# Layer norm at the end of a graph network with experts: subtraction of the mean on GpSimd, part of the normalisation on VectorE, unequal groups

## The chip, the cores and the metric

The kernel runs on one core of a Trainium2 chip. The metric is the device time of one execution in microseconds (us). The engines are TensorE (PE), VectorE (DVE), ScalarE (ACT), GpSimd (POOL) and SyncE (SP), which issues most of the DMAs. Each engine works through its own queue in order and waits there for semaphores.

## The reference

One layer of a graph network: each node gathers its neighbours' rows, which are scaled by degrees and projected; a residual projection is added; a mixture of 64 experts, two for each node, is added to that; a batch norm over the nodes follows. The input is added again, and each row of 256 values is normalised. Cut to what matters here:

```python
def _layernorm(x, axis=-1, eps=1e-05):
    m = jnp.mean(x, axis=axis, keepdims=True)
    v = jnp.var(x, axis=axis, keepdims=True)
    return (x - m) / jnp.sqrt(v + eps)
...
    y = x + core                       # x: 6250 nodes of 256, core: the experts' part
    mean = jnp.mean(y, axis=0)
    var = jnp.mean((y - mean) ** 2, axis=0)
    return (y - mean) * jax.lax.rsqrt(var + BN_EPS) * gamma + beta
...
    x = _layernorm(x + _L0_gnn_ref(x, ...), axis=-1)
```

## The kernel before

The 6250 nodes lie in SBUF as 50 tiles (NT) of 125 partitions (TP) and 256 values (D), all in single precision: `x` is [125, 50, 256] and holds the layer's state, and `fb` of the same shape holds the layer's input. The kernel counts degrees and projects (to about 250 us), gathers and sums over edges (to about 1,240 us), routes to experts, runs the experts (to 1,890 us) and then the final stage. All stages but the last are the same before and after the change.

Some lines of the earlier stages appear in the prediction, since GpSimd and VectorE work at the same time there:

- L218 (VectorE, `hot_hi` and `hot_lo`): comparisons that build one-hot tables in bf16 from two tensors in SBUF.
- L338 and L432 (GpSimd, `hrow`): the difference of two 256-element rows per partition in SBUF.
- L449 to L451 (GpSimd, `mf`) and L454 to L457 (VectorE, `nmis`, `okd`): masks over edges, and two values that are reduced.
- L512, L544 and L576 (VectorE): comparisons with one or two scalars per partition.
- L956 (VectorE, `b1c`): a copy of four elements per partition for each expert.
- L1204 (GpSimd, `fb`): while the experts run, `beta` is added to `fb`, four tiles at a time, with beta's row repeated over the tiles.

The final stage is under a manual schedule: each engine runs its instructions in the order in which the program writes them. First, every two tiles, the experts' rows are loaded, VectorE adds them to `x` (L1248), ScalarE squares (L1251), and TensorE sums rows and squares over the nodes (L1253, L1255). From these sums VectorE makes `scale` (gamma over the deviation) and `less` (mean times scale), rows of 256 values that are the same on every partition (L1257 to L1267).

What follows is the part that is changed. The batch norm and the second residual are `x * scale + (fb - less)`; beta is in `fb` already. Before the change ten groups of five tiles go through three functions:

- `sums`: VectorE multiplies five tiles of `x` by `scale` (L1274), subtracts `less` from five tiles of `fb` (L1275), and adds the two tile by tile with the row sum as a second result (L1278). L1280 turns the sums `lm` into minus the row's mean.
- `squares`: ScalarE squares each row with the mean taken off and sums it (L1287), then takes a root for all five (L1289), `ssq`.
- `rows_out`: VectorE takes reciprocals (L1294) and the products with the means (L1295); ScalarE writes the normalised rows into the tile `o` (L1298); SyncE stores `o` in two DMAs, of 112 and of 13 partitions (`node_dma`, L139 to L141).

`rows_out` of a group stands behind `squares` of the next group. `o` comes from a pool of two buffers, `lm` and `ssq` have three.

Of the kernel before, what the change touches and what calls it, by code (L numbers as in the profile page):

```python
# [15 lines left out]
AF = mybir.ActivationFunctionType  # L16
ALU = mybir.AluOpType
# [7 lines left out]
TP = 125  # L25
NT = N // TP
D = 256
# [94 lines left out]
def gnn_moe_kernel(ctx, tc, x_in, src, dst, bases, firsts, slots, W_gc, b_gc, W_res, b_res, Wg, bg, w1, b1, w2, b2,  # L122
                   gamma, beta, out):
    nc = tc.nc
    V, S, G, T = nc.vector, nc.scalar, nc.gpsimd, nc.tensor
# [6 lines left out]
    def node_rows(ap, t0, n):  # L132
        return ap[t0 * TP:(t0 + n) * TP, :].rearrange("(t p) d -> p t d", p=TP)

    def node_dma(eng, to_sbuf, tile_ap, rows):

        for a, b in ((0, 112), (112, TP)):
            if to_sbuf:
                eng.dma_start(out=tile_ap[a:b], in_=rows[a:b])  # L139
            else:  # L140
                eng.dma_start(out=rows[a:b], in_=tile_ap[a:b])  # L141
# [55 lines left out]
    with tc.tile_pool(name="edges", bufs=1) as ep, ExitStack() as later:  # L197
# [30 lines left out]
        with tc.tile_pool(name="deg", bufs=1) as dp, tc.tile_pool(name="hot", bufs=2) as hp, \  # L228
# [52 lines left out]
            for a, b in ((0, HEAD), (HEAD, NGR)):  # L281
                floor_div(hi[:, a:b], srcf[:, a:b], TP)
                V.scalar_tensor_tensor(lo_b[:, a:b], hi[:, a:b], -float(TP), srcf[:, a:b], op0=ALU.mult,
                                       op1=ALU.add)
# [201 lines left out]
        with tc.tile_pool(name="cnt", bufs=1) as cp, tc.tile_pool(name="rows", bufs=1) as rp, \  # L486
# [44 lines left out]
            groups = [(c, j, i) for c, (g0, k, w, n) in enumerate(DENSE) for j in range(n) for i in range(k)]  # L531
# [219 lines left out]
            now, n = 0.0, 0  # L751
# [18 lines left out]
            with tc.For_i(0, n_groups, 1) as gi:  # L770
# [4 lines left out]
                                op1=ALU.mult)  # L775
# [3 lines left out]
                                       op0=ALU.mult, op1=ALU.add)  # L779
# [53 lines left out]
    x = xpool.tile([TP, NT, D], F32, name="x")  # L833
# [42 lines left out]
    with tc.tile_pool(name="xw", bufs=1) as xw, tc.tile_pool(name="xl", bufs=3) as xl, \  # L876
# [23 lines left out]
        with tc.manual_schedule():  # L900
            sums = {}
            for t0 in range(ta, tb, 2):
                n = min(2, tb - t0)
# [5 lines left out]
            for t0, z in sums.items():  # L909
                n = min(2, tb - t0)  # L910
# [6 lines left out]
                for t in range(t0, t0 + n):  # L917
                    V.scalar_tensor_tensor(x[:, t, :], z[:, t - t0, :D], s_in[:, t - t0:t - t0 + 1], x[:, t, :],
                                           op0=ALU.mult, op1=ALU.add)
# [7 lines left out]
            for a, b in ((0, ta), (tb, NT)):  # L927
                for t0 in range(a, b, 10):
                    n = min(10, b - t0)
# [37 lines left out]
    for j in range(2):  # L967
        o = rt.tile([TP, E, NT], BF16, name=f"pick{j}")
# [19 lines left out]
    with tc.tile_pool(name="ps_r", bufs=1, space=PSUM) as ps_r:  # L988
# [21 lines left out]
        for e0 in range(0, E, EC):  # L1010
            n = min(EC, E - e0)
# [21 lines left out]
        for a, m, r in ((0, LA, rest), (LA, LB, rest1)):  # L1033
# [10 lines left out]
                               accum_out=lb)  # L1044
# [4 lines left out]
                               accum_out=lb)  # L1049
# [37 lines left out]
    with tc.tile_pool(name="rt2", bufs=2) as rt2, \  # L1087
# [6 lines left out]
        for t0 in range(0, NT, TB):  # L1094
            for j in range(2):
# [13 lines left out]
                for i in range(TB):  # L1109
                    t = t0 + i  # L1110
# [23 lines left out]
    fb = fpool.tile([TP, NT, D], F32, name="fb")  # L1134
# [4 lines left out]
    with tc.tile_pool(name="ex", bufs=2) as xp, \  # L1139
# [56 lines left out]
        for e, r in enumerate(turns):  # L1196
            if e % 4 == 2:
                t0 = e // 4 * 4
                n = min(4, NT - t0)
# [6 lines left out]
            if e % 4 == 0 and e // 4 * 4 < NT:  # L1206
                xs = x[:, e:min(e + 4, NT), :]
# [3 lines left out]
            c, n = r + min(r, TWO), 2 if r < TWO else 1  # L1211
# [22 lines left out]
    with tc.tile_pool(name="fin", bufs=1) as fp, tc.tile_pool(name="gat", bufs=8) as gp, \  # L1234
            tc.tile_pool(name="fl", bufs=2) as fl, \
            tc.tile_pool(name="ps_m", bufs=1, space=PSUM) as ps_m, tc.manual_schedule():
        eps = fp.tile([TP, 2], F32, name="eps")
        V.memset(eps, LN_EPS)

        S.activation(eps[:, 1:2], eps[:, 0:1], AF.Sqrt)  # L1240
        pm = ps_m.tile([TP, D], F32, name="pm")
        pv = ps_m.tile([TP, D], F32, name="pv")
        for t0 in range(0, NT, 2):
            yr = gp.tile([TP, 2, 2, D], F32, name="yr")
            node_dma(nc.sync, True, yr.rearrange("p t j d -> p t (j d)"), node_rows(y_rows, t0, 2))
            for t in range(t0, t0 + 2):
                for j in range(2):
                    V.scalar_tensor_tensor(x[:, t, :], yr[:, t - t0, j, :], gates[:, j, t:t + 1], x[:, t, :],  # L1248
                                           op0=ALU.mult, op1=ALU.add)
            sq = fl.tile([TP, 2, D], F32, name="sq", bufs=4)  # L1250
            S.activation(sq, x[:, t0:t0 + 2, :], AF.Square)  # L1251
            for t in range(t0, t0 + 2):
                T.matmul(pm, ones[:TP, :TP], x[:, t, :], start=(t == 0), stop=(t == NT - 1))  # L1253
            for t in range(t0, t0 + 2):
                T.matmul(pv, ones[:TP, :TP], sq[:, t - t0, :], start=(t == 0), stop=(t == NT - 1))  # L1255
        mean = fp.tile([TP, D], F32, name="mean")
        V.tensor_scalar(mean, pm, 1.0 / N, None, op0=ALU.mult)  # L1257
        msq = fp.tile([TP, D], F32, name="msq")
        V.tensor_mul(msq, mean, mean)
        scale = fp.tile([TP, D], F32, name="scale")  # L1260
        V.scalar_tensor_tensor(scale, pv, 1.0 / N, msq, op0=ALU.mult, op1=ALU.subtract)
        V.tensor_scalar(scale, scale, 0.0, BN_EPS, op0=ALU.max, op1=ALU.add)
        S.activation(scale, scale, AF.Sqrt)
        V.reciprocal(scale, scale)  # L1264
        V.tensor_mul(scale, scale, gam)
        less = fp.tile([TP, D], F32, name="less")
        V.tensor_mul(less, mean, scale)  # L1267


        part = {}  # L1270

        def sums(t0):
            xs, fs = x[:, t0:t0 + 5, :], fb[:, t0:t0 + 5, :]
            V.tensor_tensor(xs, xs, scale[:, None, :].to_broadcast([TP, 5, D]), ALU.mult)  # L1274
            V.tensor_tensor(fs, fs, less[:, None, :].to_broadcast([TP, 5, D]), ALU.subtract)  # L1275
            lm = fl.tile([TP, 5], F32, name="lm", bufs=3)
            for t in range(5):
                V.scalar_tensor_tensor(xs[:, t, :], xs[:, t, :], 1.0, fs[:, t, :], op0=ALU.mult, op1=ALU.add,  # L1278
                                       accum_out=lm[:, t:t + 1])
            V.tensor_scalar(lm, lm, -1.0 / D, None, op0=ALU.mult)  # L1280
            part[t0] = lm

        def squares(t0):
            ssq = fl.tile([TP, 5], F32, name="ssq", bufs=3)
            for t in range(5):
                sq = fl.tile([TP, D], F32, name="sq2")
                S.activation(sq, x[:, t0 + t, :], AF.Square, bias=part[t0][:, t:t + 1],  # L1287
                             accum_out=ssq[:, t:t + 1])
            S.activation(ssq, ssq, AF.Sqrt, scale=1.0 / D, bias=eps[:, 0:1])  # L1289
            part["ssq", t0] = ssq  # L1290

        def rows_out(t0):
            rs, lm = part.pop(("ssq", t0)), part.pop(t0)
            V.reciprocal(rs, rs)  # L1294
            V.tensor_mul(lm, lm, rs)  # L1295
            o = fl.tile([TP, 5, D], F32, name="o")
            for t in range(5):
                S.activation(o[:, t, :], x[:, t0 + t, :], AF.Identity, scale=rs[:, t:t + 1], bias=lm[:, t:t + 1])  # L1298
            node_dma(nc.sync, False, o, node_rows(out, t0, 5))

        for t0 in range(0, NT, 5):
            sums(t0)
            squares(t0)
            if t0:
                rows_out(t0 - 5)
        rows_out(NT - 5)


_INS = ["x", "src", "dst"] + ["L0_gnn_" + n for n in (
# [44 lines left out]
```

## Time and profile before

| What | Before |
|---|---|
| Time, median of 3 runs | 2028.05 us (2023.2 to 2032.3) |
| The profiled execution: its time | 2020.97 us |
| The profiled execution: its span | 2019.2 us |
| Busy: PE, DVE, ACT, POOL | 1623.9, 1105.0, 756.7, 1024.7 us |
| First L1274 starts | 1954.31 us |
| Last L1298 ends (ACT) | 2013.96 us |

Times in the profile are counted from the span's start. The span is a little shorter than the time of the same execution, which has work around it, and this execution was faster than the median of the runs. A row of a group gives line, engine, operation, output and inputs with shapes, the count, and then busy time, the mean duration of one in ns, and the idle time before them. A row of the timeline gives start, duration, engine, line, operation; the brackets at its end give the idle time of the engine before it and what ended that. A row of the chain gives start, length and the piece of work. A row of busy times by stage gives the stretch, its length, the busy time of PE, weight loads, DVE, ACT and POOL, the granted clock of TensorE, the share of DMA and GB/s.

### The profile page before, as it was taken

Reading aid. Unit: us, or ns where it says so; the run is one execution under the profiler, and the core shown is the slowest. Engines: PE = TensorE matmul, PEld = TensorE weight load, DVE = VectorE, ACT = ScalarE, POOL = GpSimd, SP = SyncE. Lnnn points to the kernel's source line nnn. Section 1 sums busy time; section 2 is a strip of 40 time slices with the busy share of each in tenths; the row PEclk is TensorE's granted clock in tenths of the full one; section 3 lists DMA queues with packets and bytes.
Section 4 is the critical chain, followed back from the end, with each engine's and each line's share of the span. In section 5 each row is a group of like instructions: output and inputs, shape, how many; then the busy total and the mean of one; then the engine's idle time right before and its main releaser. Section 6 shows DMA issues by size and latency. Waiting matters only on the chain. (4 is left out here: it accounts for less than half of the span.)

```text
span 2019.2 us, 31796 instructions
## 1 busy us (share of the span) xinstructions
PE 1623.9 (80%) x10841; PEld 1359.8 (67%) x10841; DVE 1105.0 (55%) x2689; ACT 756.7 (37%) x1844; POOL 1024.7 (51%) x1099
## 2 busy tenths in 40 slices
PE   4999588888888888888878886359989999999760
PEld 2555457777777777878777775247778887778640
DVE  7999786665665654555554543983212221212497
ACT  1443554344434444444444442022222222223238
POOL 3433447667676666666656673015555555444100
PEclk9999679999999999998989987579999999999885
DMA  4765766777777776777766764907878887779754
GB/s 134 202 183 173 232 178 177 210 203 196 197 203 219 196 209 196 208 196 210 201 198 193 210 189 119 198 22 227 243 227 250 259 263 231 239 231 323 206 130 127
DMA packets 237970, 404.23 MB, mean 200 GB/s; under 512 B 26247, under 2 KB 155671, under 8 KB 237803
## 3 DMA queue, kind: packets, MB, share of 16 engines
q0 software_dynamic: 63584, 201.44, 35.3%
q1 hardware_dynamic: 166657, 193.19, 32.5%
q10 hardware_dynamic: 7562, 7.52, 1.4%
q8 instruction: 87, 1.43, 0.3%
q14 instruction: 80, 0.66, 0.1%
HBM read 324.36 MB, written 77.68 MB: 199 GB/s over the span
## 5 line engine op out<-in xcount | busy, mean ns | idle before, releaser
L502 POOL DMA_INDIRECT r<-h_dram,srcg x631 | 648.8, 1028 | 327.4 <-issue 114.2
L572 PE MATMUL sm<-hrow,counts 125*126 125x258 f32 (+2 forms) x1600 | 512.8, 338 | 4.9 <-issue 4.8
L573 PE MATMUL sm<-hrow,counts 125*126 125x256 f32 (+2 forms) x1600 | 436.1, 290 | 2.7 <-issue 2.5
L544 DVE TENSOR_SCALAR hotk<-iota_h,key 128x350 bf16<-128x350 f16 (+6 forms) x932 | 257.3, 315 | 324.6 <-PE pc L553 152.1
L557 ACT CAST stage<-pc 128x350 f16<-128x350 f32 (+6 forms) x666 | 278.4, 450 | 413.2 <-PE pc L553 210.0
L572 PEld LDWEIGHTS sm<-hrow,counts 125*126 125x126 f32 (+2 forms) x1600 | 321.5, 201 | 71.5 <-issue 65.2
L553 PE MATMUL pc<-hotk,lo 128*128 128x350 bf16 (+6 forms) x932 | 273.3, 333 | 68.2 <-issue 48.9
L573 PEld LDWEIGHTS sm<-hrow,counts 125*126 125x126 f32 (+2 forms) x1600 | 319.2, 200 | 3.7 <-issue 2.6
L1180 ACT ACTIVATE hT<-ph,b1c 128x256 f32<-128x256 f32 (+1 forms) x320 | 136.2, 429 | 395.6 <-PE ph L1178 217.7
L1178 PE MATMUL ph<-xgT,w1s 128*128 128x256 f32 (+1 forms) x1280 | 254.5, 346 | 25.9 <-DVE xgT L1173 13.2
L1178 PEld LDWEIGHTS ph<-xgT,w1s 128*128 128x128 f32 x1280 | 202.5, 192 | 71.4 <-ACT hT L1180 21.5
L1184 PE MATMUL py<-w2s,hT 128*128 128x256 f32 x1008 | 236.2, 384 | 5.0 <-ACT hT L1180 3.2
L507 PE MATMUL pg<-r,hot 128*128 128x258 f32 x631 | 212.6, 337 | 24.2 <-issue 9.7
L1188 POOL DMA_INDIRECT y_dram<-ys,dest x126 | 123.9, 983 | 175.5 <-DVE ys L1187 134.4
L1184 PEld LDWEIGHTS py<-w2s,hT 128*128 128x128 f32 x1008 | 189.9, 192 | 33.5 <-ACT hT L1180 5.5
L1168 POOL DMA_INDIRECT xg<-x_dram,ids x126 | 123.0, 976 | 160.6 <-DVE ids L1123 93.8
L508 PE MATMUL pg<-r,hot 128*128 128x256 f32 x631 | 183.1, 290 | 2.1 <-issue 1.9
L956 DVE COPY b1c<-b1T 128x4 f32 x80 | 17.7, 221 | 251.7 <-ACT hT L1180 214.0
L507 PEld LDWEIGHTS pg<-r,hot 128*128 128x128 f32 x631 | 127.1, 201 | 41.8 <-issue 17.6
L1187 DVE TENSOR_TENSOR ys<-py,b2s 128x256 f32<-128x256 f32 x126 | 53.4, 425 | 155.8 <-PE py L1184 121.4
L218 DVE TENSOR_TENSOR hot_lo<-lo_b,iota 128x4096 bf16<-128x4096 bf16 x49 | 130.9, 2671 | 0.0
L508 PEld LDWEIGHTS pg<-r,hot 128*128 128x128 f32 x631 | 126.9, 201 | 2.6 <-issue 1.5
(317 smaller groups left out, 2114.8 us busy)
## 6 DMA issues: line engine op xcount, KB each, us to landing
w1s<-in_L_gnn_w_dram SPq DMA_DIRECT2D x80, 512.0 KB
w2s<-in_L_gnn_w_dram SPq DMA_DIRECT2D x80, 512.0 KB
y_dram<-zeros SPq DMA_DIRECT2D x48, 256.0 KB
yr<-y_dram SPq DMA_DIRECT2D x25, 448.0 KB
b2s<-in_L_gnn_b_dram SPq DMA_DIRECT2D x80, 128.0 KB
r<-h_dram,srcg POOLq DMA_INDIRECT x631
h_dram<-hrow SPq DMA_DIRECT2D x5, 1344.0 KB
z_dram<-zeros ACTq DMA_DIRECT2D x7, 903.0 KB
```

Of the source, the lines that this page charges most:

```text
L218: V.tensor_tensor(o, pairs(t, c0, n, m), iota_2[:, None, :m, :].to_broadcast([128, n // 2, m, 2]), ALU.is_equal)
L502: G.indirect_dma_start(out=f32(r[:, :2 * D]), out_offset=None, in_=h_dram[:, :], in_offset=bass.IndirectOffsetOnAxis(ap=idx, axis=0))
L507: T.matmul(pg, hot, r[:, D:], start=first, stop=False)
L508: T.matmul(pg[:, :D], hot, r[:, :D], start=False, stop=last)
L544: V.tensor_scalar(hots[g], iota_h[:, :NT * w], key[:, g:g + 1], None, op0=ALU.is_equal)
L553: T.matmul(live["pc"], los[g // PAIRS][:, r // 2, :, r % 2], hots.pop(g), start=(i == 0), stop=(i == k - 1))
L557: S.copy(stage[:, :, j * w:(j + 1) * w], live["pc"])
L572: T.matmul(sm[:m], by, hrow[:, t, D:], start=(t == 0), stop=False)
L573: T.matmul(sm[:m, :D], by, hrow[:, t, :D], start=False, stop=(t == NT - 1))
L1178: T.matmul(ph[:, :m], w1s[:, kk, c * 128:(c + 1) * 128], xgT[:, kk, :m], start=(kk == 0), stop=(kk == 1))
L1180: S.activation(hT[:, c, :m], ph[:, :m], AF.Gelu, bias=b1_e[:, c:c + 1])
L1184: T.matmul(py, hT[:, c, k * 128:(k + 1) * 128], w2s[:, c, :], start=(c == 0), stop=(c == 3))
```

## The change

The groups have 2, 3, then eight times 5, then 3 and 2 tiles. The subtraction of `less` goes to GpSimd, and all twelve groups' subtractions are queued there at the start. The multiplication by `scale` of a group is written a group ahead of its sums. In a group, tiles with an odd number (two of five, one of three, one of two) are normalised on VectorE, the others on ScalarE as before. Nothing else differs.

```diff
-        def sums(t0):
-            xs, fs = x[:, t0:t0 + 5, :], fb[:, t0:t0 + 5, :]
-            V.tensor_tensor(xs, xs, scale[:, None, :].to_broadcast([TP, 5, D]), ALU.mult)
-            V.tensor_tensor(fs, fs, less[:, None, :].to_broadcast([TP, 5, D]), ALU.subtract)
+        groups, t0 = [], 0
+        for n in [2, 3] + [5] * ((NT - 10) // 5) + [3, 2]:
+            groups.append((t0, n))
+            t0 += n
+        assert t0 == NT
+
+        def residual(t0, n):
+            fs = fb[:, t0:t0 + n, :]
+            G.tensor_tensor(fs, fs, less[:, None, :].to_broadcast([TP, n, D]), ALU.subtract)
+
+        def scaled(t0, n):
+            xs = x[:, t0:t0 + n, :]
+            V.tensor_tensor(xs, xs, scale[:, None, :].to_broadcast([TP, n, D]), ALU.mult)
+
+        def sums(t0, n):
             lm = fl.tile([TP, 5], F32, name="lm", bufs=3)
-            for t in range(5):
-                V.scalar_tensor_tensor(xs[:, t, :], xs[:, t, :], 1.0, fs[:, t, :], op0=ALU.mult, op1=ALU.add,
-                                       accum_out=lm[:, t:t + 1])
+            for t in range(n):
+                V.scalar_tensor_tensor(x[:, t0 + t, :], x[:, t0 + t, :], 1.0, fb[:, t0 + t, :], op0=ALU.mult,
+                                       op1=ALU.add, accum_out=lm[:, t:t + 1])
...
-        def rows_out(t0):
+        def rows_out(t0, n):
             rs, lm = part.pop(("ssq", t0)), part.pop(t0)
-            V.reciprocal(rs, rs)
-            V.tensor_mul(lm, lm, rs)
+            V.reciprocal(rs[:, :n], rs[:, :n])
+            V.tensor_mul(lm[:, :n], lm[:, :n], rs[:, :n])
             o = fl.tile([TP, 5, D], F32, name="o")
-            for t in range(5):
-                S.activation(o[:, t, :], x[:, t0 + t, :], AF.Identity, scale=rs[:, t:t + 1], bias=lm[:, t:t + 1])
-            node_dma(nc.sync, False, o, node_rows(out, t0, 5))
-
-        for t0 in range(0, NT, 5):
-            sums(t0)
-            squares(t0)
-            if t0:
-                rows_out(t0 - 5)
-        rows_out(NT - 5)
+            for t in range(n):
+                if t % 2:
+                    V.tensor_scalar(o[:, t, :], x[:, t0 + t, :], rs[:, t:t + 1], lm[:, t:t + 1], op0=ALU.mult,
+                                    op1=ALU.add)
+                else:
+                    S.activation(o[:, t, :], x[:, t0 + t, :], AF.Identity, scale=rs[:, t:t + 1],
+                                 bias=lm[:, t:t + 1])
+            node_dma(nc.sync, False, o[:, :n, :], node_rows(out, t0, n))
+
+        for t0, n in groups:
+            residual(t0, n)
+        scaled(*groups[0])
+        for i, g in enumerate(groups):
+            if i + 1 < len(groups):
+                scaled(*groups[i + 1])
+            sums(*g)
+            squares(*g)
+            if i:
+                rows_out(*groups[i - 1])
+        rows_out(*groups[-1])
```

`squares` differs only in that it runs over n tiles.

More of the change, by code (lines that the diff above doesn't have):

```diff
@@ L1270, in gnn_moe_kernel, with squares @@
         part = {}
-        def sums(t0):
-            xs, fs = x[:, t0:t0 + 5, :], fb[:, t0:t0 + 5, :]
-            V.tensor_tensor(xs, xs, scale[:, None, :].to_broadcast([TP, 5, D]), ALU.mult)
-            V.tensor_tensor(fs, fs, less[:, None, :].to_broadcast([TP, 5, D]), ALU.subtract)
+        groups, t0 = [], 0
[10 more added lines that the diff above has]
+        def sums(t0, n):
             lm = fl.tile([TP, 5], F32, name="lm", bufs=3)
-            for t in range(5):
-                V.scalar_tensor_tensor(xs[:, t, :], xs[:, t, :], 1.0, fs[:, t, :], op0=ALU.mult, op1=ALU.add,
-                                       accum_out=lm[:, t:t + 1])
-            V.tensor_scalar(lm, lm, -1.0 / D, None, op0=ALU.mult)
+            for t in range(n):
+                V.scalar_tensor_tensor(x[:, t0 + t, :], x[:, t0 + t, :], 1.0, fb[:, t0 + t, :], op0=ALU.mult,
+                                       op1=ALU.add, accum_out=lm[:, t:t + 1])
+            V.tensor_scalar(lm[:, :n], lm[:, :n], -1.0 / D, None, op0=ALU.mult)
             part[t0] = lm
-        def squares(t0):
+        def squares(t0, n):
             ssq = fl.tile([TP, 5], F32, name="ssq", bufs=3)
-            for t in range(5):
+            for t in range(n):
                 sq = fl.tile([TP, D], F32, name="sq2")
@@ L1288, in squares @@
                              accum_out=ssq[:, t:t + 1])
-            S.activation(ssq, ssq, AF.Sqrt, scale=1.0 / D, bias=eps[:, 0:1])
+            S.activation(ssq[:, :n], ssq[:, :n], AF.Sqrt, scale=1.0 / D, bias=eps[:, 0:1])
             part["ssq", t0] = ssq
-        def rows_out(t0):
+        def rows_out(t0, n):
             rs, lm = part.pop(("ssq", t0)), part.pop(t0)
-            V.reciprocal(rs, rs)
-            V.tensor_mul(lm, lm, rs)
+            V.reciprocal(rs[:, :n], rs[:, :n])
+            V.tensor_mul(lm[:, :n], lm[:, :n], rs[:, :n])
             o = fl.tile([TP, 5, D], F32, name="o")
-            for t in range(5):
-                S.activation(o[:, t, :], x[:, t0 + t, :], AF.Identity, scale=rs[:, t:t + 1], bias=lm[:, t:t + 1])
-            node_dma(nc.sync, False, o, node_rows(out, t0, 5))
-        for t0 in range(0, NT, 5):
-            sums(t0)
-            squares(t0)
-            if t0:
-                rows_out(t0 - 5)
-        rows_out(NT - 5)
+            for t in range(n):
+                if t % 2:
[16 more added lines that the diff above has]
+        rows_out(*groups[-1])
 _INS = ["x", "src", "dst"] + ["L0_gnn_" + n for n in (
```

## The prediction

> **What bounds the kernel now.** I read the chain that ended last first, because only its last stretch runs through the changed lines; then busy times by stage; then, for the work that moves to GpSimd, the groups by form and the timeline at places where GpSimd and VectorE ran together. The first fence is from the chain (start, length, piece). One round of five tiles on VectorE goes from 1993.32 to 1998.54, 5.22 us; one round on ScalarE from 1985.26 to 1990.51, 5.25 us. The chain hops between two engines that are equally long.
>
> ```profile
> 1985.26 2.47 ACT sq L1287 x10
> ...
> 1987.75 0.04 ACT ssq L1289
> ...
> 1987.95 2.55 ACT o L1298 x5
> 1990.51 2.47 ACT sq L1287 x10
> ...
> 1993.32 1.83 DVE x L1278 x10
> 1995.17 0.17 DVE lm L1280
> 1995.34 0.10 DVE ssq L1294
> 1995.46 0.17 DVE lm L1295
> 1995.63 1.40 DVE x L1274
> 1997.03 1.42 DVE fb L1275
> ```
>
> The stages say the same: in 30 us VectorE works 29.06 and ScalarE 29.67, GpSimd nothing, and DMA has room (share 0.38).
>
> ```profile
> 1964.00:1994.00 30.00, 0.00 (x0) 0.00 (x0) 29.06 (x83) 29.67 (x93) 0.00 (x0) 0.50 0.38 107
> ```
>
> So the stage (first L1274 at 1954.31 to the span's end at 2019.2, 64.9 us) gets shorter only if both engines lose work and nothing takes its place. The question is what the idle engine charges. Its nearest rows, by form:
>
> ```profile
> L1204 POOL TENSOR_TENSOR fb<-fb,bet 125x1024 f32<-125x1024 f32 x12 | 28.2, 2354 | 12.7 <-DMA fb<-in_x_dram 12.6
> L1204 POOL TENSOR_TENSOR fb<-fb,bet 125x512 f32<-125x512 f32 x1 | 1.3, 1260 | 5.9 <-DMA fb<-in_x_dram 5.9
> ```
>
> It is the same shape of operation, with a row repeated over tiles: (2354 - 1260) / 512 = 2.14 ns per element and 0.17 us fixed. And the timeline shows what VectorE does meanwhile:
>
> ```profile
> 227.39 3.48 POOL L451 TENSOR_TENSOR mf<-mf,dstf 128x1568 f32<-128x1568 f32 x1
> 227.51 0.15 DVE L456 TENSOR_SCALAR okd<-okd 128x1 f32<-128x1 f32 x1
> 227.70 3.19 DVE L457 TENSOR_TENSOR nmis<-nmis,okd 128x1 f32<-128x1 f32 x1
> ...
> 96.00 0.98 DVE L218 TENSOR_TENSOR hot_hi<-hi_b,iota 128x1600 bf16<-128x1600 bf16 x1
> 96.37 1.20 POOL L338 TENSOR_TENSOR hrow<-whole,hrow 125x256 fp32r<-125x256 f32 x1 [2.44 <-ACT whole L337]
> 96.90 2.82 DVE L218 TENSOR_TENSOR hot_lo<-lo_b,iota 128x4096 bf16<-128x4096 bf16 x1
> ```
>
> L457 subtracts one element per partition from another and takes 3.19 us: it ends at 230.89, when GpSimd's L451 ends (230.87). L456, without a second tensor, passes in 0.15. In the second piece GpSimd's L338 takes 1.20 us, where its twin L432 has a median of 0.73 in a quieter stage: it stands until hot_hi ends at 96.98, then runs to 97.57, and hot_lo, started at 96.90, is stretched. With the rounds 3.55 and 3.64 us long in turn, and 0.90 for hot_hi and 2.20 for an undisturbed hot_lo (shortest 2.28, less the 0.08 by which neighbours overlap), one 256-element instruction on GpSimd costs VectorE 0.45 to 0.54 us. Two tensor operations of two SBUF inputs, one on each engine, exclude each other.
>
> **The change, part by part**, on the profiled execution (span 2019.2, time 2020.97; the median of the runs is 2028.05, and I add the difference of spans to that median).
>
> *VectorE's own work.* The fb subtraction leaves: 5.22 - 1.42 = 3.80 us per five tiles, 38.0 for fifty. Twelve groups in place of ten repeat twice what a group pays whatever its size: reciprocal and product 0.29, the scaling of lm with the gaps around the sums 0.38, a start 0.08; 1.5 in all. Twenty tiles are normalised here (two of five, one of two, one of three). The trace has no 256-element row with two scalars per partition. Below stands L1262 (two constants, 0.29, so 0.21 apart when overlapped), above L1248 (one scalar and a second tensor, 0.45 apart); L576, two scalars per partition on 128 elements, has a mean of about 0.34-0.38. I take 0.35, near L576: 7.0 (4.2 to 9.0). Sum 46.5 us, against 52.2 for ten rounds now.
>
> *ScalarE.* Fifty squares of 0.494, twelve roots at about 0.30 with their gaps, thirty normalisations of 0.493: 24.7 + 3.6 + 14.8 = 43.1 against 52.5 now. It stays just below VectorE's 46.5.
>
> *GpSimd.* Twelve subtractions over 12,800 elements per partition: 27.4 us of streaming and 12 x 0.17 = 2.0 fixed, 29.4 altogether. If it ran beside VectorE all of it would be free: it has nothing else here, and the first residual (1.26) is covered by the two scalings ahead (0.6 + 0.9). But x times scale (L1274) and the sums (L1278) read two SBUF tensors each, like L457 and hot_lo. So the streaming is added to VectorE's line. Its price there: L338's 0.45 to 0.54 per 256 elements gives 22.5 to 27; no hiding gives 29.4; no exclusion gives 0. I take 27.4 less about 0.1 for each of twelve hand-overs, in which VectorE's parts without a second tensor pass: 26.2. It is nearest to the row of L451 and L457, where the hold was complete.
>
> The Trainium skill, page "SBUF — State Buffer", section "Who interferes with whom", speaks against this change: it says that the port pair which GpSimd and VectorE share is held for the whole instruction. By that rule the term would be an estimated 29.4, and the sum 3.2 higher; the L338 rows say that a little of each instruction is free.
>
> *Order.* All residuals are queued at once, so they do not wait for VectorE's data, only for the port. L338 got in between two VectorE instructions, so I expect turns: for some 27 + 6 = 34 us one two-input instruction of VectorE per residual, the third group barely begun, ScalarE mostly idle. It can't make that up later: from the third group on it has about 40 of its 43 us left, which just fits behind 1988 in VectorE's line and the tail below.
>
> *The ends.* VectorE's line: 1954.31 + 46.5 + 26.2 = 2027.0. The last sums end before the normalisation work of the last two groups (2 x 0.65): 2025.7, against 2005.8 now. After that now: 13.4 us. Then: squares of two tiles 1.0, root 0.3, normalisations 1.5, gaps 0.6, and a store that is shorter: the span ends 5.2 us after ScalarE's last row (2013.96), of which three fifths of 2.7 us traffic go, leaving 3.6. Together 7.0. One new wait: `o` has two buffers, so the final two-tile group writes the buffer of the last five-tile group, whose store isn't done. Three of that group's rows (1.5 us with a gap 1.6) still stand on ScalarE when the last sums end; now traffic ends 3.5 us after the rows, and I add 1.0 for completion (0 to 1.7, by the span's end); then half a microsecond for the last row and 3.6 for its store: 1.6 + 4.5 + 0.5 + 3.6 = 10.2. I take that; without the wait it is 7.0.
>
> Sum: 2025.7 + 10.2 = 2035.9, 16.7 later than 2019.2. By parts: VectorE's own work -5.7, the port +26.2, the tail -3.2, and -0.6 because 1.3 of VectorE's line now lies behind the last sums where 0.7 does so today. Forecast: 2028.05 + 16.7 = 2044.8 us.
>
> **Rivals.** *A, no exclusion for these operations, so not slower.* Price: the 26.2 go away; 2009.7 for the span, -9.5, 2018.6. For it: no row has two long fp32 instructions of this kind at once. Against: L457 is an fp32 subtraction of two SBUF tensors and stood still; L956, a copy of 4 elements that normally takes 0.17, took 2.13 under the first L1204. It decides the sign where a GpSimd tile costs VectorE under 9.5 / 50 = 0.19 us; measured are 0.45 to 0.54. *B, GpSimd keeps the port through its whole queue*: VectorE stands for 29.4 with nothing hidden; +19.9, 2047.9. For it: L449, L450 and L451 follow each other within 0.1 us. Against: the turns at L338. *C, half the price* (0.25 per tile, 12.5): +3.0, 2031.1, if single-precision sums leave gaps that GpSimd can fill; no row shows such gaps.
>
> **How the numbers follow.** A measurement of this kernel can tell about 0.5%, 10 us, from no change: faster is below 2017.9, slower above 2038.2. Chances: forecast 0.70, B 0.13, C 0.06, A 0.11. The forecast's own range takes the low prices together (port 22.5, normalisations 4.2, no buffer wait: +7.0, 2035) to the high ones (29.4, 9.0: +22, 2050). The runs before lie 9 us apart, so I widen it to 2032 to 2052, which takes in B; A, most of C and scatter are left out, about 0.2. Slower: 0.60 of the forecast and B, 0.73. Same: 0.10 of the forecast, C and half of A, 0.21. Faster: the rest of A, 0.06.
>
> **What would show it.** Right: residuals on GpSimd stretched over some 34 us with a mean clearly above 2.9 us for five tiles; L1278 and L1274's successors with single instructions of about 3 us in that stretch and 0.42 and 1.48 afterwards; ScalarE with long waits for lm until about 1988, then rounds of 4.3 to 4.5 us; a wait of 2 to 3 us before the last rows for the store. Wrong: residuals at 2.9 us on end beside sums of 0.42 us (A), VectorE at rest for 29 us on end (B), normalisations on VectorE far from 0.4 us, or ScalarE rounds above 4.6 us.

## The result and the profile after

The changed kernel takes 2052.19 us (median of 4 runs, 2045.39 to 2062.23), the kernel before 2028.33 on the same chip: a ratio of 1.0102, interval 1.0066 to 1.0139. In us that is 20.7 slower, 13 to 28 (the two medians lie 23.9 apart); 16.7 had been forecast. The profiled execution has a span of 2049.8 us against 2019.2, 30.6 more, and that difference has two parts. The first multiplication by `scale` starts at 1968.3 instead of 1954.3, so 14.0 us were lost ahead of the final stage, where both kernels run the same program. The final stage itself, from that instruction to the span's end, takes 81.5 us against 64.9: 16.6 us longer.

The busy times of the final stage, in three stretches (columns as before: length, PE, weight loads, DVE, ACT, POOL, clock, DMA share, GB/s):

```profile
1968.30:2002.00 33.70, 0.00 (x0) 0.00 (x0) 33.56 (x23) 3.87 (x13) 33.31 (x12) 0.50 0.03 8
2002.00:2038.30 36.30, 0.00 (x0) 0.00 (x0) 34.03 (x137) 34.07 (x112) 0.00 (x0) 0.50 0.41 117
2038.30:2049.80 11.50, 0.00 (x0) 0.00 (x0) 2.96 (x13) 6.12 (x19) 0.00 (x0) 0.50 0.59 167
```

For 33 us GpSimd and VectorE both count as busy all the time, and yet VectorE gets 23 instructions done and ScalarE works for under 4 us. In the next 36 us VectorE does 137. An engine that is busy by the profile may be standing inside an instruction; the counts tell. The groups by form show where (first one of the kernel before, then those of the change):

```profile
L1278 DVE SCALAR_TENSOR_TENSOR x<-x,fb 125x256 f32<-125x256 f32 x50 | 18.1, 423 | 0.8
```

```profile
L1289 DVE SCALAR_TENSOR_TENSOR x<-x,fb 125x256 f32<-125x256 f32 x50 | 31.5, 686 | 0.0
L1280 POOL TENSOR_TENSOR fb<-fb,less 125x1280 f32<-125x1280 f32 x8 | 25.0, 3152 | 0.0
L1284 DVE TENSOR_TENSOR x<-x,scale 125x1280 f32<-125x1280 f32 x8 | 13.5, 1683 | 0.0
L1310 DVE TENSOR_SCALAR o<-x,ssq,lm 125x256 f32<-125x256 f32 x20 | 10.1, 537 | 5.6 <-DMA out_dram<-o 5.2
```

The mean of the sums is 0.69 us where it was 0.42, and a five-tile subtraction takes 3.15 us where 2.9 had been worked out for GpSimd alone. The timeline of the first stretch tells how a mean of 0.69 comes about:

```profile
1968.43 33.31 POOL L1280 TENSOR_TENSOR fb<-fb,less 125x512 f32<-125x512 f32 x12 [62.99 <-DVE less L1267]
...
1975.89 2.72 DVE L1291 TENSOR_SCALAR lm<-lm 125x2 f32<-125x2 f32 x1
...
1979.92 3.09 DVE L1289 SCALAR_TENSOR_TENSOR x<-x,fb 125x256 f32<-125x256 f32 x1
...
1982.95 3.08 DVE L1289 SCALAR_TENSOR_TENSOR x<-x,fb 125x256 f32<-125x256 f32 x1
...
1991.72 0.15 DVE L1305 RECIPROCAL ssq<-ssq 125x2 f32<-125x2 f32 x1
1991.91 2.73 DVE L1306 TENSOR_TENSOR lm<-lm,ssq 125x2 f32<-125x2 f32 x1
1994.68 2.94 DVE L1310 TENSOR_SCALAR o<-x,ssq,lm 125x256 f32<-125x256 f32 x1
...
2006.00 0.42 DVE L1289 SCALAR_TENSOR_TENSOR x<-x,fb 125x256 f32<-125x256 f32 x1
```

Turns are taken: one VectorE instruction, one subtraction of GpSimd, and so on. A sum is 3.1 us long while the queue of subtractions lasts and 0.42 us afterwards. A product of two elements per partition (L1306) takes 2.73 us. The reciprocal passes in 0.15.

The end of the chain that ended last:

```profile
2040.03 1.58 ACT o L1313 x3
...
2041.98 3.65 DMA out_dram<-o
...
2045.74 0.60 ACT o L1313
```

The last row of the two-tile group waits for the store of the last five-tile group, as the prediction said.

### The profile page after: what moved, and what is told of

Read it like the earlier page. It is cut to its first block, busy times and chain, and to the rows that moved or that the text cites. A ratio compares the mean times of both kernels' runs of the same rounds, so it can differ in the third digit from the quotient of the medians.

```text
span 2049.8 us, 31830 instructions
## 1 busy us (share of the span) xinstructions
PE 1627.2 (79%) x10841; PEld 1365.5 (67%) x10841; DVE 1123.2 (55%) x2707; ACT 747.1 (36%) x1826; POOL 1058.1 (52%) x1111
## 5 line engine op out<-in xcount | busy, mean ns | idle before, releaser
L956 DVE COPY b1c<-b1T 128x4 f32 x80 | 16.7, 209 | 239.3 <-ACT hT L1180 194.2
L1187 DVE TENSOR_TENSOR ys<-py,b2s 128x256 f32<-128x256 f32 x126 | 53.2, 425 | 164.6 <-PE py L1184 118.9
```

## The experiments

X is the theory of the prediction: GpSimd's subtractions and VectorE's instructions exclude each other, and that costs VectorE some 26 us. "Stage" is the final stage as above. The runs were made on several chips, and on three of them the stage that gathers over edges is so much shorter that whole times lie some 150 us lower; so I compare stages across chips, and times only with the kernel before on the same chip.

| Kernel | Stage, us | Time over before on its chip (interval) |
|---|---|---|
| before, and again on another chip | 64.9, 64.9 | |
| the change, and again on another chip | 81.5, 81.5 | 1.0102 (1.0066 to 1.0139), 1.0062 (1.0039 to 1.0084) |
| no_residual | 55.3 | |
| residual_on_vector | 68.4 | 1.0026 (1.0003 to 1.0049) |
| memset_instead | 55.3 | |
| normalise_on_gpsimd | 65.0 | 0.9984 (0.9964 to 1.0004) |
| own_last_buffer | 80.9 | |
| small_ends_only | 67.1 | 1.0007 (0.9988 to 1.0026) |
| residual_on_pe | 121.1 | 1.0308 (1.0274 to 1.0341) |
| pe_one_row | 94.2 | |
| pe_all_rows | 55.0 | 0.9940 (0.9920 to 0.9960) |
| pe_all_rows_ones | 55.3 | 0.9935 (0.9916 to 0.9954) |

**Is the loss in the final stage? (change_again, before_again; both without an edit)**

> The changed kernel once more, beside the variants below and on the same chip as they. Its first profile lost 16.6 us in the final stage (81.5 against 64.9 us) and 14 us ahead of it, where the program is the same. Theory X: the stage is 81.5 us again, the earlier part differs only by chance, and the time is 15 to 19 us over before. Rival E (the change also lengthens the earlier stages): 20 to 31 us over before, with the stage's start later than in other kernels of the same chip.

> The kernel before, profiled on the chips of the later runs, where it takes some 150 us less than in the first ones. Both theories: the stage is 64.9 us here too, since nothing in it depends on what made the earlier stages faster; a stage other than 64 to 66 us would spoil the comparison of stages between chips.

Both stages come out the same to 0.1 us on other chips: 81.5 and 64.9. The chip of before_again, at 2009 us, is not one of those three, so that for them the 64.9 is carried over and not measured; the change's 81.5 was measured on one of them. Nothing in the profiles ties the 14 us ahead of the stage to the change. On the second chip the change is 11.6 us slower (7.3 to 15.8, from the ratio and 1877 us), on the first 20.7 (13 to 28), and the stages differ by 16.6. The rival E, by which the earlier stages suffer too, falls on the second chip. The 11.6 lies below the 15 to 19 that X expected, and that its interval ends a little below 16.6 is left open; the runs of before there spread over 15 us, and no run separates the earlier stages from chance.

**The subtraction alone (no_residual, residual_on_vector)**

```diff
-        for t0, n in groups:
-            residual(t0, n)
         scaled(*groups[0])
```

> The changed kernel without the subtraction of less on any engine (the result is left unsubtracted): the whole price of that step by itself. Theory X: the stage is VectorE's line alone, 46.5 - 1.3 + 10.2 = 55.4 us, 26 below the changed kernel's 81.5; sums at 0.42 us throughout. Rival R: above 70 us, since order and normalisations remain.

Measured: 55.3. All of the 26.2 us between this and 81.5 is the subtraction on GpSimd, and it is the term of the prediction to the tenth. The order and the normalisations on VectorE, which R blames, are still there. The second kernel puts the subtraction on VectorE:

```diff
-            G.tensor_tensor(fs, fs, less[:, None, :].to_broadcast([TP, n, D]), ALU.subtract)
+            V.tensor_tensor(fs, fs, less[:, None, :].to_broadcast([TP, n, D]), ALU.subtract)
...
-        for t0, n in groups:
-            residual(t0, n)
         scaled(*groups[0])
+        residual(*groups[0])
...
                 scaled(*groups[i + 1])
+                residual(*groups[i + 1])
```

> The changed kernel with the subtraction of less back on VectorE, a group ahead beside the scaling; all else as in the change. By 'stage' I mean the time from the start of the first multiplication by scale to the span's end: 64.9 us before, 81.5 in the changed kernel. Theory X (GpSimd's tensor instructions and VectorE's exclude each other, so the subtraction costs VectorE 26 us from GpSimd and 14.2 on VectorE itself): VectorE's line 46.5 + 14.2 = 60.7, last sums at 59.4, tail 10.2, stage 69.6, no sums instruction above 0.45 us, time about 5 us over before. Rival R (the loss lies in the new order and in the twenty normalisations on VectorE, not in GpSimd): stage stays above 78 us.

Measured: 68.4. Its groups by form:

```profile
L1289 DVE SCALAR_TENSOR_TENSOR x<-x,fb 125x256 f32<-125x256 f32 x50 | 18.2, 421 | 0.0
L1280 DVE TENSOR_TENSOR fb<-fb,less 125x1280 f32<-125x1280 f32 x8 | 11.9, 1485 | 0.0
L1310 DVE TENSOR_SCALAR o<-x,ssq,lm 125x256 f32<-125x256 f32 x20 | 7.5, 411 | 4.7 <-DMA out_dram<-o 4.3
```

The engine that is already full does the step for 68.4 - 55.3 = 13.1 us; the idle one charges 26.2 for it, to the full one. Against before, this kernel is still 3.5 us longer in the stage. The normalisations that came to VectorE on top are not all of it: small_ends_only, further down, has none of them there and is still 2.2 longer.

**What excludes what (memset_instead, normalise_on_gpsimd)**

```diff
-            G.tensor_tensor(fs, fs, less[:, None, :].to_broadcast([TP, n, D]), ALU.subtract)
+            for _ in range(2):
+                G.memset(fs, 0.0)
```

> GpSimd writes zeros into fb (each group twice, to last roughly as long as the subtraction) instead of subtracting less, so the residual is left out of the result; queue, order and dependences are those of the change, but GpSimd reads no SBUF. Theory X in the form 'both engines read two tensors': sums keep 0.42 us beside the writes, and only instructions with one tensor input of SBUF in and out (the scaling of lm, the normalisations) may be held; stage 55 to 62 us. Rival W (any work of GpSimd in SBUF holds VectorE's tensor instructions): sums stretched to the length of a write, stage about 55.4 + 25 = 80 us.

Measured: 55.3, the stage of no subtraction at all. But this says nothing about W, since the kernel didn't put GpSimd's writes where they were meant to be. A memset reads no `less`, so nothing held it back until the stage. A row of the source view gives the count, the shortest, median and longest in ns, and the first and last start:

```profile
L1281 POOL MEMSET fb<- x24: 524/1164/1190, 1267.6 to 1581.9; 125x1280 f32 x16, 125x512 f32 x4, 125x768 f32 x4
```

All 24 ran while the experts ran, the last of them 226 us ahead of the stage, which starts at 1808.1. In the stage GpSimd did nothing, and the run is no_residual once more. What the memsets did to VectorE can be seen where they stood, in the timeline of the expert stage:

```profile
1374.24 2.40 POOL L1281 MEMSET fb<- 125x1280 f32 x2
1374.26 1.20 DVE L956 COPY b1c<-b1T 128x4 f32 x1 [2.08 <-ACT hT L1180]
1375.59 0.42 DVE L1187 TENSOR_TENSOR ys<-py,b2s 128x256 f32<-128x256 f32 x1
```

L956, a copy of one tensor with a median of 0.17 us, stands until the first of the two memsets ends (it ends at 1375.46; half of the 2.40 is over at 1375.44). Six of these copies met a memset and took 0.37 to 1.60 us. L1187, which adds a tensor of PSUM and one of SBUF, keeps its 0.42 beside the second. So GpSimd's writing alone does hold a copy with one tensor. Whether it would hold the sums, which read two tensors of SBUF, no run shows, since none of them met a memset; that it is GpSimd's reading that holds them is not shown.

The other kernel gives GpSimd a reader with one tensor: subtraction on VectorE as above, own buffer as below, and

```diff
                 if t % 2:
-                    V.tensor_scalar(o[:, t, :], x[:, t0 + t, :], rs[:, t:t + 1], lm[:, t:t + 1], op0=ALU.mult,
+                    G.tensor_scalar(o[:, t, :], x[:, t0 + t, :], rs[:, t:t + 1], lm[:, t:t + 1], op0=ALU.mult,
```

> Subtraction on VectorE, the odd tiles of a group normalised on GpSimd in place of VectorE (one tensor and two scalars per partition), own buffer for the two-tile groups. ScalarE has 43 us, VectorE 53.7 of its own. Theory X1 (any GpSimd instruction that reads SBUF excludes VectorE's two-input ones): VectorE's instructions stretch beside it, 20 x 0.27 to 0.43 us more, stage 66 to 70. Rival X2 (only two tensor inputs on both sides exclude each other): sums keep 0.42 us, stage 60 to 62.

Measured: 65.0, between the two, and neither holds as put. GpSimd's row among its groups by form:

```profile
L1310 POOL TENSOR_SCALAR o<-x,ssq,lm 125x256 f32<-125x256 f32 x20 | 36.8, 1848 | 86.9 <-DVE lm L1306 77.6 <-issue 5.1 <-ACT sq L1298 2.9
```

And of the timeline of VectorE, two sums beside them:

```profile
1840.10 0.61 DVE L1289 SCALAR_TENSOR_TENSOR x<-x,fb 125x256 f32<-125x256 f32 x1
...
1840.64 0.41 DVE L1289 SCALAR_TENSOR_TENSOR x<-x,fb 125x256 f32<-125x256 f32 x1
```

The sums that meet it are longer by 0.19 us, 3.0 in all (21.2 for the fifty against 18.2 in residual_on_vector), and GpSimd's own instructions wait: the shortest took 0.55 us, the longest 3.23. X2 falls, since the sums beside a reader with one tensor don't keep their 0.42. X1 holds in kind, at about half the price that it gave: 0.19 is less than the 0.55 that the shortest takes, so the sum doesn't stand for all of it. The price over twenty tiles is small enough that the kernel comes out even with before.

**The ends (own_last_buffer, small_ends_only)**

```diff
-            o = fl.tile([TP, 5, D], F32, name="o")
+            o = fl.tile([TP, 5, D], F32, name="o") if n > 2 else fl.tile([TP, 2, D], F32, name="o2", bufs=1)
```

> The change with a buffer of its own for the rows of the two-tile groups, so that the last rows need not wait for the store of the last five-tile group. Theory T (the wait is a term of the tail): no wait of the last rows, which are done 2.4 us sooner; the stores then queue one behind the other, so the stage shortens by 1.0 to 2.4 us, to 79 to 80.5. Rival: stores alone set the end, stage stays at 81.5.

Measured: 80.9, so 0.6 us are won, less than T expected and more than the rival. The last group no longer waits and its rows are done 2.0 us sooner, but the three-tile group before it still waits (1.88 us for the store of the group two ahead of it), and the stores follow each other: in this kernel DMA is busy almost without a break from 1882.5 to 1887.3 us, as it is in the change from 2042.5 to 2046.2. The truth lies between the two: the wait is a term, and the stores take most of what it gives.

small_ends_only is residual_on_vector with this edit and with all rows normalised on ScalarE.

> The division of work of before (subtraction on VectorE, all normalisations on ScalarE, GpSimd idle) with the change's unequal groups, its order and a buffer of its own for the two-tile groups: the unequal ends alone. By the prediction's terms: two more groups cost VectorE 1.5, line 53.7, last sums at 53.0 after the stage's start (51.5 before); the tail of squares 1.0, root 0.3, rows 2.5, gaps 0.4 and store 3.6 is 7.8 in place of 13.4; stage 60.8 against 64.9, time 4 us under before, if the ends are worth what the prediction says. Rival: the two extra groups and the serial stores eat it, stage 64 to 66.

Measured: 67.1 and no change in time. My sum followed VectorE and forgot whom it feeds. The first row is from the waits of the kernel before, the others from this one (who waited for whom: us in total, times, longest):

```profile
ACT sq L1287 <- DVE lm L1280: 9.5, 2, 7.6
```

```profile
ACT sq L1298 <- DVE lm L1291: 11.9, 4, 6.6
DVE ssq L1305 <- ACT ssq L1300: 5.7, 3, 3.4
```

ScalarE waits 11.9 us for row means, where it waits 9.5 before. Ahead of the first group it waits less, 6.6 against 7.6, but after it each small group is used up while VectorE scales and subtracts the larger one that follows. Once ScalarE has no more to wait for, the chain stays on it to the end: it has 53.2 us of work, as full an engine as VectorE with 51.3. With both engines full, groups of unequal size and work a group ahead cost at the start at least what they save at the end.

**Another idle engine (residual_on_pe, pe_all_rows, pe_all_rows_ones, pe_one_row).** TensorE does nothing in the stage and its result lies in PSUM. The first form, two tiles to a bank:

```diff
+            pf = ps_f.tile([TP, 2, D], F32, name="pf")
+            for t in range(2):
+                T.matmul(pf[:, t, :], ident[:TP, :TP], fb[:, 2 * p + t, :], start=True, stop=False)
+                T.matmul(pf[:, t, :], minus, less[0:1, :], start=False, stop=True)
...
-                V.scalar_tensor_tensor(x[:, t0 + t, :], x[:, t0 + t, :], 1.0, fb[:, t0 + t, :], op0=ALU.mult,
+                V.scalar_tensor_tensor(x[:, t0 + t, :], x[:, t0 + t, :], 1.0, summed[(t0 + t) // 2][:, (t0 + t) % 2, :], op0=ALU.mult,
```

> TensorE forms fb - less in PSUM (identity times fb plus minus one times less, two tiles to a bank, six banks ahead), and the sums read it from there; GpSimd does nothing in the stage, all else as in the change. Theory X: VectorE's line is 46.5 us again, TensorE's 100 matmuls of 256 columns at 0.38 us are 38 us beside it, stage 55.4 to 58 us, 7 to 9.5 us below before. Rival P (TensorE becomes the bound: it wakes at half clock, where the same shape took 0.79 us): up to 79 us of matmuls and a stage of 80 to 90 us.

Measured: 121.1; the rival P, and worse than it said. Each of the 100 products shows as two matmuls in the trace, 200 in all, and the clock fell: the first matmul of one row starts at 1804.94. By stage:

```profile
1805.00:1806.00 1.00, 1.00 (x4) 0.52 (x4) 1.00 (x2) 0.00 (x0) 0.00 (x0) 1.00 0.00 0
1807.00:1808.00 1.00, 1.00 (x3) 0.49 (x2) 0.56 (x3) 0.00 (x0) 0.00 (x0) 0.50 0.00 0
...
1830.00:1860.00 30.00, 30.00 (x54) 12.87 (x53) 10.51 (x40) 9.30 (x30) 0.00 (x0) 0.50 0.20 56
```

TensorE is busy for all of it, is granted 1.00 at first and 0.50 from about 1807 on. The sums, 0.42 us, don't mind that one input comes from PSUM. The next form:

```diff
+            T.matmul(pf, ident[:TP, :TP], fb[:, 2 * p:2 * p + 2, :], start=True, stop=False)
...
+            T.matmul(filled[p], ident[:TP, :TP], less[:, None, :].to_broadcast([TP, 2, D]), start=False, stop=True)
...
-        V.tensor_mul(less, mean, scale)
+        V.scalar_tensor_tensor(less, mean, -1.0, scale, op0=ALU.mult, op1=ALU.mult)
```

> As residual_on_pe, but the part with minus less is also a matmul of all 125 rows (identity times minus less), both parts take two tiles at once (512 columns), and the identity part of the first twelve tiles is queued right behind the sums over nodes, so that TensorE has no pause; own buffer for the two-tile groups. In residual_on_pe the granted clock was 0.50 through the whole stage although TensorE was busy all the time, and half of its matmuls had one row. Theory C1 (the one-row matmuls kept the clock down): clock 1.0, 50 tiles x 0.86 = 43 us, beside VectorE's 46.5; stage 55 to 58 us against 64.9, time 7 to 9 us under before. Rival C2 (the clock falls in this stage whatever the matmuls are): TensorE's rate as in residual_on_pe, stage 95 to 120.

> As pe_all_rows, but the second part multiplies a matrix of ones by minus less over 125, so that every weight of half of the matmuls counts and the weights change between parts. C1: clock 1.0 and a stage of 55 to 58 us here too. If the identity's zeros keep the clock down, this one is fast and pe_all_rows slow. C2: both slow, 95 to 120.

Measured: 55.0 and 55.3, faster than before by 0.6% and 0.65% (11 and 12 us, where the stage is 9.9 and 9.6 shorter), clear of noise. pe_all_rows by stage:

```profile
1813.40:1823.40 10.00, 10.00 (x24) 4.32 (x23) 9.18 (x33) 3.97 (x14) 0.00 (x0) 1.00 0.09 24
1823.40:1843.40 20.00, 20.00 (x48) 8.80 (x47) 19.54 (x72) 19.68 (x67) 0.00 (x0) 1.00 0.40 113
```

And two of its groups by form:

```profile
L1293 PE MATMUL pf<-less,ident 125*125 125x512 f32 x50 | 24.7, 593 | 0.0
L1303 DVE SCALAR_TENSOR_TENSOR x<-x,pf 125x256 f32<-125x256 f32 x50 | 17.9, 416 | 0.6 <-PE pf L1293 0.6
```

The clock is 1.00 and three engines are full at once. Since three things had changed between the two forms, the last kernel puts one of them back:

```diff
-            T.matmul(filled[p], ident[:TP, :TP], less[:, None, :].to_broadcast([TP, 2, D]), start=False, stop=True)
+            T.matmul(filled[p], minus, less[0:1, None, :].to_broadcast([1, 2, D]), start=False, stop=True)
```

> pe_all_rows with one thing put back: the second part is a matmul of one row again (minus one times less). Two tiles at once, the early identity parts and the own buffer stay. C1 (one-row matmuls keep the clock down): granted clock near 0.50 in the stage, TensorE bound, stage above 90 us. Rival C3 (the pause before less, or the 256-column steps, were the cause in residual_on_pe): clock 1.0, stage 55 to 56 as in pe_all_rows.

```profile
1938.00:1940.00 2.00, 2.00 (x6) 0.78 (x5) 1.17 (x7) 0.13 (x1) 0.00 (x0) 1.00 0.00 0
...
1946.50:1966.50 20.00, 20.00 (x21) 4.92 (x20) 11.27 (x39) 11.56 (x40) 0.00 (x0) 0.50 0.19 55
```

Measured: 94.2. The identity parts ran ahead without a pause at a clock of 1.00; the first matmul of one row starts at 1937.71, and from 1940 on the clock is 0.50, on the same chip and with TensorE busy throughout. C1 is shown, C2 and C3 fall: a matmul of one row in place of 125, half of all, halves the clock of a TensorE that doesn't rest. That pe_all_rows and pe_all_rows_ones agree shows that zeros among the weights of the second part don't matter.

## Why the prediction was right

*VectorE's line.* Predicted: last sums 71.4 us after the stage's start. Measured: the last one ends at 2039.6, 71.3 after it. The port's term of 26.2 is the 81.5 - 55.3 of no_residual. The rows that carried it were L338 beside hot_lo, and L451 beside L457; the change's own rows repeat both patterns.

*The rule of the whole instruction.* By the Trainium skill, page "SBUF — State Buffer", section "Who interferes with whom", the subtractions would have cost an estimated 29.4; measured 26.2. The exclusion is there as the page says, and by these numbers a little of each instruction lies outside it, though no run separates that part. The same section has two-input instructions of VectorE contend with a GpSimd instruction that reads SBUF and not with one that only writes it. No run here shows the second half: in memset_instead no instruction of VectorE with two inputs from SBUF met a memset.

*Order.* The subtractions took 33.3 us (34 expected), in turns, and ScalarE's rounds afterwards are 4.1 us once and then 4.3 to 4.5. One thing was misjudged: the scaling of lm and the normalisation have one tensor input, and I let the like of them pass beside GpSimd as L456 does. They took turns as well (2.72 and 2.94 us); the reciprocal did pass, in 0.15. It moved which instruction stood when. But the 1.2 us that I took off the term rested on such instructions passing at the hand-overs, so that the 26.2 was hit to the tenth is luck, within the 22.5 to 29.4 that the rows allowed. B falls with the turns, A and C with the 26.2.

*VectorE's and ScalarE's work.* A normalisation on VectorE measures 0.41 us and 0.33 to the next start, against 0.35; no_residual's 55.3 stands against 55.4 from the sum without the port.

*The tail.* Predicted 10.2, measured 10.2 (2039.6 to 2049.8), with the wait for the buffer in its place. But own_last_buffer shows that the 7.0 without that wait was wrong: 0.6 us are won, not 3.2, because the stores stand in line behind one another. The number was right with a cause that is only one of two, and that is luck.

*The time.* 16.7 was the difference of the stages, and it came out at 16.6. The first chip's 20.7 and the second's 11.6 stand on both sides of it. The median of 2052.19 is 7.4 above the forecast of 2044.8 and 0.2 past the upper end of its range: the profiled execution lost 14 us ahead of the stage, for which the sum has no term and which no run ties to the change.

## What to carry to other kernels

Before work goes to an idle engine, look in the trace for places where that engine and the full one ran at once, and price the step by what the full one lost there, not by the idle one's own time. Here GpSimd's estimated 29 us were 26 us of VectorE's; TensorE did the same step for nothing, once all its rows were in use. And of two engines that are equally full, relieving one (normalise_on_gpsimd, 65.0 us) or making its groups smaller (small_ends_only, 67.1) moved nothing here: count each one's line, and who feeds whom at the start.

## What was not expected of the hardware

- With one-row matmuls as half of all, the granted clock fell from 1.00 to 0.50 within about 2 us and stayed there for as long as TensorE was busy, 105 us (residual_on_pe) and 81 us (pe_one_row); with 125 rows it stayed at 1.00 (pe_all_rows).
- GpSimd that only writes SBUF holds a copy of VectorE with one tensor: four elements per partition took up to 1.60 us beside a memset, against 0.17 (memset_instead). And GpSimd's subtraction held instructions with one tensor input, 2.72 and 2.94 us.
- While GpSimd and VectorE take turns, an instruction on two elements per partition waits as long as one on 256: 2.73 and 3.08 us. Small instructions are the dearest to have beside a long one.
